# 5x5 depthwise sums in PSUM instead of SBUF, the padded images filled by ACT, and gathers of 128 rows instead of 126

## The chip, the cores and the metric

One core of a Trainium2 chip runs the whole program. The metric is the device time of one execution in microseconds; the median of several unprofiled and profiled executions is quoted. TensorE is PE below, VectorE DVE, ScalarE ACT, GpSimd POOL, SyncE SP.

## The reference, cut to what matters

Four images of 256 channels and 64x64 points go through four residual layers, each after a group norm:

```python
# layer 0: conv 1x1, depthwise 3x3 -> offsets and masks; 36 bilinear samples per point (4 groups x 9 points),
#          weighted sum, projection, squeeze-excite, fc1/fc2
samp = _grid_sample(img, sg)
dout = (samp * mr).sum(-1) ...
# layer 1: linear attention on q, k, v and on their 5x5 depthwise aggregation
qkv = relu(conv1x1(x) * scale + bias)                        # 768 channels
agg = conv2d(qkv, agg_dw_w, [(2, 2), (2, 2)], groups=C3) + agg_dw_b[None, :, None, None]
agg = conv2d(agg, agg_pw_w, groups=C3) + agg_pw_b
ms = concatenate([qkv, agg]);  vk = v @ k^T;  out = vk @ q / (sum(k) . q + eps);  proj, relu
# layer 2: binary 3x3 convolution        # layer 3: non-local attention with pooled keys
```

Layer 0's sampling is done by indirect DMAs (gathers) that POOL issues, each fetching one table row of 1 KB per partition. Layer 1's 5x5 aggregation is done by DVE: 25 multiply-adds of 128x1024 elements for each of 24 sums per image (here called accumulations: 2,400 in all, of which 2,304 are `scalar_tensor_tensor`; the first of each sum is a `tensor_scalar`). While image n is sampled, the remaining layers of image n-1 run beside it.

## The kernel before

The parts that the change and the argument touch:

```python
def depthwise(self, acc, src, w, k, rows, cols, r0, bias=None):
    for t in range(k * k):
        s = src[:, r0 + t // k:r0 + t // k + rows, t % k:t % k + cols]
        wt = w[:, t:t + 1]
        if t:
            nc.vector.scalar_tensor_tensor(acc, s, wt, acc, ALU.mult, ALU.add)
        elif bias is not None:
            nc.vector.tensor_scalar(acc, s, wt, bias, ALU.mult, ALU.add)
        ...

def sample(self, n, ssum):                       # 74 units an image, a unit is up to 4 rounds
    ...
            wm = self.gp.tile([P, UR, 4 * G, OB], F32, name="wm")        # bufs=2: weights of a unit
            ... nc.vector.tensor_tensor(wm[0:k, v0:v1], self.con("own")[0:k]..., sl[0:k, u + v0:u + v1, G:]..., ALU.mult)
            acc = self.ps2.tile([P, UR, P], F32, name="acc", tag="ps2")
            for v, (r, m) in enumerate(unit):
                k = m * PT                                               # 14 points x 9 = 126 rows
                g = self.gp.tile([P, G, 256], F32, name="g", bufs=8)
                for i in range(G):
                    nc.gpsimd.indirect_dma_start(out=g[0:k, i, :], ..., in_=table, in_offset=... sl.bitcast(I32)[0:k, r, i:i + 1])
                ... matmuls acc <- wm[0:k], g[0:k]
            ...
            yield 1

# layer 1
    def padded(tiles, b_loop): ...               # qkv, 8 blocks an image
            nc.scalar.activation(v, ps, AF.Relu, ...)
            nc.vector.tensor_copy(pd[:, 2 + 8 * b:10 + 8 * b, 2:W + 2], rw(v))
    def aggregate(pd, i, c, name):
        acc = bp.tile([P, 16, W], F32, name=name, tag=name)              # SBUF, "ak" or "av", bufs=2
        self.depthwise(acc, pd, self.w5[:, i], 5, 16, W, 16 * c, bias=self.b5[:, i:i + 1])
        return acc
    ...
        for c in range(4):
            ak = aggregate(kp, 2 + t, c, "ak")...; nc.scalar.activation(ak, ak, AF.Relu, ...)
            av = aggregate(vp, 4 + t, c, "av")...
            ...
            yield 56

def run(self):
    ...
        for i, _ in enumerate(self.sample(n, ssum), 1):
            while spent < i * SHARE:             # SHARE = 24: how much of the image before goes with a unit
                cost = next(before, None)
                ...
```

The order in which a built program's instructions stand on each engine is not that of the source: a scheduler at build time fixes it, from the source order and the dependencies.

## Time and profile before

| | before |
|---|---|
| unprofiled, 3 runs | 11,089.57 us median (11,062.62 to 11,095.54) |
| the profiled run that came with it | 11,979.3 us span |
| PE, DVE, ACT, POOL busy | 58%, 43%, 15%, 49% |
| sampling of images 0 to 3 | 1,751, 2,319, 2,374, 2,429 us |
| without gathers after images 1 and 2 / after image 3 | 428, 425 / 2,010 us |

The lines themselves are shown in the prediction. Read them by stage: whenever POOL is at work one image is sampled, and what the other engines do then is overlap; what lies in the stretches without POOL is paid in full.

### The profile page before, as it was taken

How to read it: one execution, taken by the hardware profiler on the slowest of the kernel's cores; microseconds unless marked ns; L12 is line 12 of the kernel's file. 1: busy time of each engine (PE TensorE's matmuls, PEld its weight loads, DVE VectorE, ACT ScalarE, POOL GpSimd, SP SyncE). 2: the span in 40 equal slices, each digit the busy share in tenths (PEclk: the TensorE clock that was granted, in tenths of full speed). 3: DMA queues.
4: the chain of work that ended last, by engine and by line, in shares of the span. 5: the costliest groups of instructions: out<-in, count | busy, mean ns of one | idle time of the engine just before them, and what ended most of it. 6: DMA issues, size and time to landing. Idle time of an engine off the chain costs nothing. (4 is left out here: it accounts for less than half of the span.)

```text
span 11979.3 us, 87750 instructions
## 1 busy us (share of the span) xinstructions
PE 6993.4 (58%) x34360; PEld 3582.5 (30%) x34360; DVE 5198.2 (43%) x6141; ACT 1794.6 (15%) x3153; POOL 5874.1 (49%) x4694
## 2 busy tenths in 40 slices
PE   3455434845466864664466866383447777832686
PEld 2222222322222342332222334242222334421235
DVE  5213200287462125256664023537657112399713
ACT  1110000111111121121111022021111012221002
POOL 1777776678764421478876350538877451000000
PEclk6665556866667887776566978596667788965698
DMA  3443433322322212322232122322232221100000
GB/s 108 123 125 102 125 95 92 96 64 73 87 67 70 65 43 81 102 66 76 77 85 83 42 75 67 107 71 60 64 84 72 65 71 42 53 0 0 0 10 14
DMA packets 687911, 838.70 MB, mean 70 GB/s; under 512 B 401289, under 2 KB 507145, under 8 KB 685705
## 3 DMA queue, kind: packets, MB, share of 16 engines
q0 software_dynamic: 299776, 604.62, 18.1%
q1 hardware_dynamic: 387720, 228.48, 6.6%
q8 instruction: 270, 4.42, 0.2%
q14 instruction: 145, 1.18, 0.0%
HBM read 731.68 MB, written 100.71 MB: 69 GB/s over the span
## 5 line engine op out<-in xcount | busy, mean ns | idle before, releaser
L411 POOL DMA_INDIRECT g<-tab,sl x4688 | 5873.4, 1253 | 4094.8 <-issue 1996.5
L418 PE MATMUL acc<-g,wm 126*32 126x128 f32 x18752 | 1600.9, 346 | 1387.6 <-issue 741.3
L418 PEld LDWEIGHTS acc<-g,wm 126*32 126x32 f32 x18752 | 819.3, 133 | 2196.3 <-issue 1272.5
L158 DVE SCALAR_TENSOR_TENSOR av<-pd,vec,av 128x1024 f32<-128x1024 f32 x1152 | 1473.0, 1279 | 2.1
L158 DVE SCALAR_TENSOR_TENSOR ak<-pd,vec,ak 128x1024 f32<-128x1024 f32 x1152 | 1470.6, 1277 | 0.5
L403 DVE TENSOR_TENSOR wm<-con,sl 126x1024 f32<-126x1024 f32 (+1 forms) x296 | 358.0, 1211 | 2150.7 <-remote 1622.4
L634 PE MATMUL ps<-xp,w 128*128 128x512 f32 x2304 | 1029.0, 606 | 12.7 <-issue 9.5
L424 PE MATMUL dp<-ident,at 128*128 128x128 f32 x1172 | 274.8, 375 | 1032.8 <-ACT at L421 646.2
L421 ACT COPY at<-acc 128x512 f32<-128x512 f32 (+1 forms) x296 | 171.8, 581 | 3525.8 <-remote 2319.9
L634 PEld LDWEIGHTS ps<-xp,w 128*128 128x128 f32 x2304 | 443.2, 194 | 575.9 <-issue 571.0
L424 PEld LDWEIGHTS dp<-ident,at 128*128 128x128 f32 x1172 | 180.0, 188 | 1180.1 <-ACT at L421 727.4
L549 PE MATMUL pt<-ident,ak 128*128 128x128 f32 x256 | 85.6, 390 | 723.6 <-ACT ak L565 723.6
L484 PE MATMUL ps<-x2f,f 128*128 128x512 f32 x1024 | 469.6, 615 | 15.1 <-ACT hm L485 11.1
L638 DVE TENSOR_TENSOR x<-x,ps 128x512 f32<-128x512 f32 x64 | 44.0, 688 | 957.3 <-PE ps L634 879.6
L490 PE MATMUL ps<-hm,f 128*128 128x512 f32 x1024 | 445.2, 593 | 0.0
L524 PE MATMUL ps<-xn,qw 128*128 128x512 f32 x768 | 393.5, 649 | 4.2 <-ACT xn L124 3.9
L431 ACT COPY dT<-dp 64x224 f32<-64x224 f32 (+1 forms) x592 | 199.4, 337 | 1268.2 <-PE dp L424 756.6
L320 PE MATMUL ps<-mw,t 128*128 128x108 f32 x512 | 129.1, 407 | 419.2 <-DVE t L142 344.2
L713 PEld LDWEIGHTS ps<-gt,pT 128*128 128x128 f32 x2048 | 310.6, 232 | 121.5 <-DVE pT L710 63.2
L696 PE MATMUL s<-ph,th 128*128 128x512 f32 x512 | 332.8, 738 | 2.3 <-issue 2.2
L708 PE MATMUL pt<-ident,pe 128*128 128x128 f32 x1024 | 161.4, 302 | 287.1 <-ACT pe L702 271.1
L713 PE MATMUL ps<-gt,pT 128*128 128x128 f32 x2048 | 306.8, 314 | 37.1 <-DVE pT L710 36.8
(190 smaller groups left out, 7610.3 us busy)
## 6 DMA issues: line engine op xcount, KB each, us to landing
g<-tab,sl POOLq DMA_INDIRECT x4688
x<-in_x SPq DMA_DIRECT2D x64, 512.0 KB
tab<-xo SPq DMA_DIRECT2D x512, 64.0 KB
y<-yc SPq DMA_DIRECT2D x32, 512.0 KB
x2f<-x SPq DMA_DIRECT2D x32, 512.0 KB
ybf<-y SPq DMA_DIRECT2D x32, 512.0 KB
out<-res SPq DMA_DIRECT2D x64, 256.0 KB
yb<-y SPq DMA_DIRECT2D x32, 504.0 KB
```

The source lines that it names most:

```text
L158: nc.vector.scalar_tensor_tensor(acc, s, wt, acc, ALU.mult, ALU.add)
L403: nc.vector.tensor_tensor(wm[0:k, v0:v1], self.con("own")[0:k].unsqueeze(1).unsqueeze(1).to_broadcast(sh), sl[0:k, u + v0:u + v1, G:].unsq ...
L411: nc.gpsimd.indirect_dma_start(out=g[0:k, i, :], out_offset=None, in_=table, in_offset=bass.IndirectOffsetOnAxis(ap=sl.bitcast(I32)[0:k, r ...
L418: nc.tensor.matmul(acc[32 * i:32 * i + 32, v, :], wm[0:k, v, 4 * i + 2 * x:4 * i + 2 * x + 2, :], g[0:k, i, x * P:(x + 1) * P], start=x == ...
L424: nc.tensor.transpose(dp[:, v].rearrange("p g s o -> p (g s o)"), at[:, v], self.ident)
L431: nc.scalar.copy(dT[hs, :, q0:q0 + m * (v1 - v0)].rearrange("p g (v o) -> p g v o", o=m), dp[hs, v0:v1, :, s, 0:m].rearrange("p v g o -> p ...
L484: nc.tensor.matmul(ps, f1[:, k, m * P:(m + 1) * P], x2[:, k], start=k == 0, stop=k == KT - 1)
L490: nc.tensor.matmul(ps, f2[:, k, m * P:(m + 1) * P], hm[:, k], start=k == 0, stop=k == 4 * KT - 1)
L524: nc.tensor.matmul(ps, qw[:, k, i * P:(i + 1) * P], xn[:, k], start=k == 0, stop=k == KT - 1)
L634: nc.tensor.matmul(ps, w[:, k, t, m * P:(m + 1) * P], xp[:, k, 8 * b + t // 3:8 * b + t // 3 + 8, t % 3:t % 3 + W], start=i == 0, stop=i = ...
L696: nc.tensor.matmul(s[:, i], tv[:, 4 * b + j], ph[:, i * 512:(i + 1) * 512], start=True, stop=True)
L713: nc.tensor.matmul(ps[:, 0:P], pT[:, m], gt[:, m], start=m == 0, stop=m == 7)
```

## The change

Its intent: beside accumulations with both inputs in SBUF a gather takes about 2.09 us where a free one takes 0.997 (the prediction has the lines, and the port on which the two are held to meet). With the sum in PSUM an accumulation has one SBUF input, which should end that. ACT, which has room, moves the sum out with the relu and fills the padded images. The PSUM banks for it come from the matmul pool (3 to 2). Gathers of 128 rows take in two rows of the next point; their product lands in an output column that is never copied out.

```diff
-        self.mm = e(tc.tile_pool(name="mm", bufs=3, space=PSUM))
+        self.mm = e(tc.tile_pool(name="mm", bufs=2, space=PSUM))
 ...
-                            out=g[0:k, i, :], out_offset=None, in_=table,
-                            in_offset=bass.IndirectOffsetOnAxis(ap=sl.bitcast(I32)[0:k, r, i:i + 1], axis=0))
+                            out=g[:, i, :], out_offset=None, in_=table,
+                            in_offset=bass.IndirectOffsetOnAxis(ap=sl.bitcast(I32)[:, r, i:i + 1], axis=0))
 ...   (wm and the matmuls likewise; s_d gets 252 rows of zeros at its end; sl is loaded for 128 rows)
-                        nc.vector.tensor_copy(pd[:, 2 + 8 * b:10 + 8 * b, 2:W + 2], rw(v))
+                        nc.scalar.copy(inner, rw(v))          # q: the relu itself writes into pd
 ...
-            def aggregate(pd, i, c, name):
+            def aggregate(pd, i, c, name, func, **more):
-                acc = bp.tile([P, 16, W], F32, name=name, tag=name)
+                acc = self.big.tile([P, 16, W], F32, name="agg", tag="big")       # bufs=1
                 self.depthwise(acc, pd, self.w5[:, i], 5, 16, W, 16 * c, bias=self.b5[:, i:i + 1])
-                return acc
+                v = bp.tile([P, 16, W], F32, name=name, tag=name)
+                nc.scalar.activation(v, acc, func, **more)
+                return v
 ...
-                    yield 56
+                    yield 28      (after the k sum, and again after the v sum)
 ...   (vk moves to a bank of ps1; the relu of the q sums goes from DVE to ACT)
```

More of the change, by code (lines that the diff above doesn't have):

```diff
@@ L194, in setup @@
         nc.vector.tensor_tensor(self.b5, self.b5, self.vec("agg_pw_b", n=6), ALU.add)
+        self.zero = cp.tile([P, TX * 2], F32, name="zero")
+        nc.vector.memset(self.zero, 0.0)
         dt = self.dp.tile
@@ L200, in setup @@
         self.x2_d = [dt([P, KT, HW], F32, name=f"x2{n}") for n in im]
-        self.s_d = [dt([HW * PT, G * 5], F32, name=f"sd{n}") for n in im]
+        self.s_d = [dt([HW * PT + 2 * RS, G * 5], F32, name=f"sd{n}") for n in im]
+        for n in im:
+            nc.sync.dma_start(self.s_d[n][HW * PT:].rearrange("(p r) f -> p (r f)", r=2), self.zero[0:RS, 0:G * 10])
         self.w2_d = dt([P, KT, 9, C], F32, name="w2")
-        self.zero = cp.tile([P, TX * 2], F32, name="zero")
-        nc.vector.memset(self.zero, 0.0)
     def binarise(self):
@@ L372, in coordinates @@
         nc.sync.dma_start(
-            self.s_d[n].rearrange("(t p q) f -> p t (q f)", p=P, q=PT)[:, c * CT:(c + 1) * CT, :],
+            self.s_d[n][0:HW * PT].rearrange("(t p q) f -> p t (q f)", p=P, q=PT)[:, c * CT:(c + 1) * CT, :],
             sd.rearrange("p t q f -> p t (q f)"))
@@ L384, in sample @@
             whole, part = np_ // RP, np_ % RP
-            rows = self.s_d[n][p0 * PT:(p0 + np_) * PT, :]
-            nc.sync.dma_start(sl[0:RS, 0:whole], rows[0:whole * RS].rearrange("(r p) f -> p r f", p=RS))
-            if part:
-                nc.sync.dma_start(sl[0:part * PT, whole], rows[whole * RS:])
+            nr = whole + (part > 0)
+            rows = self.s_d[n][p0 * PT:p0 * PT + nr * RS, :].rearrange("(r p) f -> p r f", p=RS)
+            more = self.s_d[n][p0 * PT + RS:p0 * PT + (nr + 1) * RS, :].rearrange("(r p) f -> p r f", p=RS)
+            nc.sync.dma_start(sl[0:RS, 0:nr], rows)
+            nc.sync.dma_start(sl[RS:P, 0:nr], more[0:P - RS])
             yb = sp.tile([P, KT, BP], F32, name="yb")
@@ L397, in sample @@
                 wm = self.gp.tile([P, UR, 4 * G, OB], F32, name="wm")
-                ku = unit[0][1] * PT
-                full = sum(1 for _, m in unit if m == unit[0][1])
-                for v0, v1, k in ((0, full, ku), (full, nu, unit[-1][1] * PT)):
-                    if v0 < v1:
-                        sh = [k, v1 - v0, 4 * G, OB]
-                        nc.vector.tensor_tensor(
-                            wm[0:k, v0:v1], self.con("own")[0:k].unsqueeze(1).unsqueeze(1).to_broadcast(sh),
-                            sl[0:k, u + v0:u + v1, G:].unsqueeze(3).to_broadcast(sh), ALU.mult)
+                sh = [P, nu, 4 * G, OB]
+                nc.vector.tensor_tensor(
+                    wm[:, 0:nu], self.con("own").unsqueeze(1).unsqueeze(1).to_broadcast(sh),
+                    sl[:, u:u + nu, G:].unsqueeze(3).to_broadcast(sh), ALU.mult)
                 acc = self.ps2.tile([P, UR, P], F32, name="acc", tag="ps2")
                 for v, (r, m) in enumerate(unit):
-                    k = m * PT
                     g = self.gp.tile([P, G, 256], F32, name="g", bufs=8)
@@ L411, in sample @@
                         nc.gpsimd.indirect_dma_start(
-                            out=g[0:k, i, :], out_offset=None, in_=table,
-                            in_offset=bass.IndirectOffsetOnAxis(ap=sl.bitcast(I32)[0:k, r, i:i + 1], axis=0))
+                            out=g[:, i, :], out_offset=None, in_=table,
+                            in_offset=bass.IndirectOffsetOnAxis(ap=sl.bitcast(I32)[:, r, i:i + 1], axis=0))
                     for x in range(2):
                         for i in range(G):
-                            nc.tensor.matmul(acc[32 * i:32 * i + 32, v, :], wm[0:k, v, 4 * i + 2 * x:4 * i + 2 * x + 2, :],
-                                             g[0:k, i, x * P:(x + 1) * P], start=x == 0, stop=x == 1)
+                            nc.tensor.matmul(acc[32 * i:32 * i + 32, v, :], wm[:, v, 4 * i + 2 * x:4 * i + 2 * x + 2, :],
+                                             g[:, i, x * P:(x + 1) * P], start=x == 0, stop=x == 1)
                 at = sp.tile([P, UR, P], F32, name="at")
@@ L424, in sample @@
                     nc.tensor.transpose(dp[:, v].rearrange("p g s o -> p (g s o)"), at[:, v], self.ident)
-                for v0, v1, m in ((0, full, unit[0][1]), (full, nu, unit[-1][1])):
+                full = sum(1 for _, m in unit if m == RP)
+                for v0, v1, m in ((0, full, RP), (full, nu, unit[-1][1])):
                     for s in range(2):
@@ L524, in padded @@
                             nc.tensor.matmul(ps, qw[:, k, i * P:(i + 1) * P], xn[:, k], start=k == 0, stop=k == KT - 1)
+                        inner = pd[:, 2 + 8 * b:10 + 8 * b, 2:W + 2]
+                        bn = {"bias": self.vec("qkv_b", i), "scale": self.vec("qkv_s", i)}
+                        if not b_loop:
+                            nc.scalar.activation(inner, rw(ps), AF.Relu, **bn)
+                            continue
                         v = bp.tile([P, 512], F32, name="v", tag=f"v{len(got)}")
-                        more = {"accum_out": b_loop[0][:, b:b + 1]} if b_loop and not got else {}
-                        nc.scalar.activation(v, ps, AF.Relu, bias=self.vec("qkv_b", i), scale=self.vec("qkv_s", i), **more)
-                        nc.vector.tensor_copy(pd[:, 2 + 8 * b:10 + 8 * b, 2:W + 2], rw(v))
+                        more = {} if got else {"accum_out": b_loop[0][:, b:b + 1]}
+                        nc.scalar.activation(v, ps, AF.Relu, **bn, **more)
+                        nc.scalar.copy(inner, rw(v))
                         got.append(v)
@@ L533, in padded @@
                 return dst
-            def aggregate(pd, i, c, name):
-                acc = bp.tile([P, 16, W], F32, name=name, tag=name)
+            def aggregate(pd, i, c, name, func, **more):
+                acc = self.big.tile([P, 16, W], F32, name="agg", tag="big")
                 self.depthwise(acc, pd, self.w5[:, i], 5, 16, W, 16 * c, bias=self.b5[:, i:i + 1])
-                return acc
+                v = bp.tile([P, 16, W], F32, name=name, tag=name)
+                nc.scalar.activation(v, acc, func, **more)
+                return v
             for t in range(2):
                 ks = sp.tile([P, 2, NB], F32, name=f"ks{t}")
-                vk = self.big.tile([P, 2, 512], F32, name="vk", tag="big")
+                vk = self.ps1.tile([P, 2, P], F32, name="vk", tag="vk")
                 def outer(kind, kv, vv, first, last):
@@ L553, in outer @@
                     for j in range(2):
-                        nc.tensor.matmul(vk[:, kind, 0:P], kt[:, 0, j], kt[:, 1, j],
+                        nc.tensor.matmul(vk[:, kind], kt[:, 0, j], kt[:, 1, j],
                                          start=first and j == 0, stop=last and j == 1)
@@ L563, in layer1 @@
                 for c in range(4):
-                    ak = aggregate(kp, 2 + t, c, "ak").rearrange("p r w -> p (r w)")
-                    nc.scalar.activation(ak, ak, AF.Relu, accum_out=ks[:, 1, c:c + 1])
-                    av = aggregate(vp, 4 + t, c, "av").rearrange("p r w -> p (r w)")
+                    ak = aggregate(kp, 2 + t, c, "ak", AF.Relu, accum_out=ks[:, 1, c:c + 1]).rearrange("p r w -> p (r w)")
+                    yield 28
+                    av = aggregate(vp, 4 + t, c, "av", AF.Copy).rearrange("p r w -> p (r w)")
                     for i in range(4):
@@ L569, in layer1 @@
                         outer(1, ak[:, cs], av[:, cs], c + i == 0, c + i == 6)
-                    yield 56
+                    yield 28
                 for kind in range(2):
                     j = 2 * kind + t
-                    nc.vector.tensor_tensor(ln[:, j], vk[:, kind, 0:P], self.con("bd"), ALU.mult)
+                    nc.vector.tensor_tensor(ln[:, j], vk[:, kind], self.con("bd"), ALU.mult)
                     kk = sp.tile([P, 1], F32, name=f"kk{j}")
@@ L581, in layer1 @@
                 for t in range(2):
-                    v = aggregate(qp[t], t, c, ("ak", "av")[t])
-                    nc.vector.tensor_scalar(v, v, 0.0, None, ALU.max)
-                    aq.append(v)
+                    aq.append(aggregate(qp[t], t, c, ("ak", "av")[t], AF.Relu))
                     yield 28
```

## The prediction

> **What bounds the kernel now.** I read the page's busy times first, then a table of stretches cut where the stages change, then the gathers one by one in the timeline, and last the order in which the built program's instructions stand on each engine. No engine is near full over the span:
>
> ```profile
> span 11979.3 us, 87750 instructions
> PE 6993.4 (58%) x34360; PEld 3582.5 (30%) x34360; DVE 5198.2 (43%) x6141; ACT 1794.6 (15%) x3153; POOL 5874.1 (49%) x4694
> ...
> DVE  5213200287462125256664023537657112399713
> POOL 1777776678764421478876350538877451000000
> ```
>
> POOL (the gathers of the sampling) works into the 34th slice; then one image's remaining layers run without it. The stretches (start:end, length, then busy time and count per engine: PE, PEld, DVE, ACT, POOL; clock; DMA) show the loop over the four images:
>
> ```profile
> 243.00:1994.00 1751.00, 765.73 (x5422) 396.49 (x5422) 350.11 (x461) 155.97 (x312) 1275.49 (x1172) 0.59 0.40 110
> ...
> 4741.00:7115.00 2374.00, 1461.09 (x7439) 708.36 (x7440) 1122.77 (x1241) 344.52 (x620) 1545.83 (x1172) 0.72 0.28 77
> 7115.00:7540.00 425.00, 251.67 (x1143) 174.65 (x1142) 167.72 (x289) 104.03 (x168) 0.01 (x1) 0.82 0.19 57
> 7540.00:9969.00 2429.00, 1452.99 (x7435) 705.49 (x7435) 1122.76 (x1241) 344.47 (x620) 1570.02 (x1172) 0.71 0.27 75
> 9969.00:10209.00 240.00, 175.17 (x914) 127.41 (x914) 81.06 (x159) 64.73 (x113) 0.49 (x1) 0.92 0.09 35
> 10209.00:10445.00 236.00, 223.46 (x520) 99.41 (x520) 75.11 (x115) 45.92 (x68) 0.00 (x0) 0.97 0.15 48
> 10445.00:11382.00 937.00, 399.86 (x1028) 178.93 (x1028) 810.36 (x785) 148.51 (x242) 0.00 (x0) 0.64 0.00 1
> 11382.00:11648.00 266.00, 251.31 (x580) 110.73 (x580) 23.58 (x54) 11.59 (x17) 0.00 (x0) 0.97 0.02 9
> ```
>
> Sampling image 0 takes 1751 us alone. Sampling images 1 to 3 (2319, 2374 and 2429 us) carries the previous image's feed-forward, layer 1, layer 2 and part of layer 3 along; then some 425 us finish layer 3 and prepare the next image. From 9969 on image 2's layer 3 ends (240 us), and image 3 runs alone: feed-forward 236, layer 1 937, layer 2 266, layer 3 331. So the bound changes: gathers while sampling, DVE in layer 1 (810 of 937 us), PE in layer 2.
>
> While sampling runs beside layer 1, gathers and the 5x5 sums get in each other's way:
>
> ```profile
> 5325.38 15.68 POOL L411 DMA_INDIRECT g<-tab,sl  x1 [0.59 <-PE acc L418]
> 5341.36 44.61 POOL L411 DMA_INDIRECT g<-tab,sl  x1 [0.30 <-issue]
> 5386.27 2.03 POOL L411 DMA_INDIRECT g<-tab,sl  x1 [0.30 <-issue]
> 5388.60 1.00 POOL L411 DMA_INDIRECT g<-tab,sl  x1 [0.30 <-issue]
> ...
> L411 POOL DMA_INDIRECT g<-tab,sl x4688: 952/997/56565, 243.0 to 9968.5; - x196
> L158 DVE SCALAR_TENSOR_TENSOR av<-pd,vec,av 128x1024 f32<-128x1024 f32 x1152 | 1473.0, 1279 | 2.1
> L158 DVE SCALAR_TENSOR_TENSOR ak<-pd,vec,ak 128x1024 f32<-128x1024 f32 x1152 | 1470.6, 1277 | 0.5
> ```
>
> A free gather takes 0.997 us and starts every 1.30. Beside an unbroken row of sums (start to start 1.194 us) it takes about 2.09; two of these took 15.68 and 44.61. Taking every gather's excess over 0.997 us, I get about 1,200 us over the four images. That is what the change wants back.
>
> **What the Trainium skill says.** "SBUF — State Buffer", section "Who interferes with whom": a DVE instruction with two SBUF inputs contends with a GpSimd one that reads SBUF, under an exclusive lock; one with at most one SBUF input, outside the two-port modes, does not. The gathers read their indices from SBUF, and the lines above agree. "VectorE: DVE Perf Modes", section on the TRN2 errata, gives fixed costs of 58 cycles SBUF to SBUF and 120 from PSUM, 65 ns apart at 0.96 GHz. For a PSUM source this trace hardly agrees (the 512-wide add takes 688 ns with one PSUM input, 691 without); no DVE instruction here writes PSUM. "DMA: Bandwidth & Descriptors", section on why a DMA increments its semaphore by 16, derives the engine count from the largest divisor up to 16: 126 rows would use 14 engines, 128 all 16. The trace shows only that rows matter little to POOL: the 72-row gathers took about 0.955 us, the 126-row ones 0.997.
>
> **The change part by part.**
> *Gathers of 128 rows:* 0.042 us for 54 rows makes 0.002 us a gather, 7 us in all. Transfers may land earlier; 1,172 gathers at 1.30 us would still be 1,524 us an image. I count nothing.
> *Filling the padded images on ACT:* 192 DVE copies of 0.43 us go (82 us), and 32 relu passes of 0.68 (22). ACT has room.
> *Sums in PSUM:* 2,304 accumulations lose their second SBUF input, so the lock goes. For each I take 1.25 us from start to start: 1.194, some 0.025 because one chain replaces two alternating ones (the 3x3 chain runs at 1.21 to 1.23), and half of the skill's 65 ns. There is one two-bank accumulator, so at each of 24 sums per image DVE waits for ACT to empty it: 1.06 us measured for ACT's 1024-wide relu, some 1.5 with both hand-overs, 36 us an image.
> *One matmul bank fewer:* feed-forward has two matmuls to one eviction and stays PE-bound; I count nothing apart.
> *Order:* this decides. DVE is in-order, and each unit of sampling (16 gathers) has one weight build (wm) on DVE that cannot run until the matmuls of two units earlier are done. Before, the scheduler puts 20 accumulations between two wm in the first part of layer 1 (199 in 8 units of image 2), so sampling and layer 1 advance together. In the changed program, only five:
>
> ```
> 645 L402 TensorTensor wm<-con,sl 128x1024
> 646 L158 TensorScalarPtr agg<-pd,vec,agg 128x1024 x5
> 647 L402 TensorTensor wm<-con,sl 128x1024
> ```
>
> For image 1's sampling I count 305 accumulating instructions of 600 before the last wm; 295, and every matmul of den, num, layer 2 and layer 3, come after it. It is the same for the next two. A unit then offers 5 x 1.25 + 1.2 = 7.5 us of DVE work to 16 gathers that need at least 20.8: DVE must wait for POOL at every wm, and half of layer 1 and two whole layers fall out of the overlap.
>
> *Sum,* in microseconds of the profiled run. Sampling alone ran 320 gathers in 464.9 us (from 1407.8 on), 1.453 each; I use 1.45 where only five accumulations run beside it.
> - Image 0 ends at 1994, as before.
> - Image 1: the first 192 gathers, beside feed-forward, take 383 as before; 980 x 1.45 = 1421; together 1804. What is left of image 0: 295 x 1.25 = 369 of accumulation, 13 evictions 19, other DVE work 70, PE's trailing part and waits about 60, together 520; layer 2 266; layer 3 331; then preparation 182 (4559 to 4741 before, and after layer 3 in both orders). 1804 + 1299 = 3103, before 2747.
> - Image 2: its first 192 gathers took 473; 473 + 1421 + 1299 = 3193, before 2799.
> - Image 3: 473 + 1421 = 1894, then 1117 for the rest of image 2.
> - Last image alone: 236 + 987 + 266 + 331 = 1820, where layer 1's 937 gets 39 for PSUM and 36 for evictions, and loses 25 of copies and relu.
> Total 1994 + 3103 + 3193 + 1894 + 1117 + 1820 = 13,121 against 11,979: 1.095 times. The unprofiled runs take 11,090; with the same ratio, about 12,150.
>
> **The rivals.**
> *The freed port wins.* Suppose layer 1 still went along with sampling as before. By the start of every 128th gather of image 2, the 40 units from 5215 to 6422 took 1,207 us; with DVE (199 x 1.25 + 8 x 1.2 = 258 us) as the bound of the first eight and gathers at 1.45 us (186) as that of the other thirty-two they would take 258 + 4 x 186 = 1,002. That is 205 an image, 615 in all: 11,364 profiled, 10,520 unprofiled, faster by 5%. For it: the blocked gathers. Against it: the order is fixed in the program, and the built order of the kernel before agrees with its trace for all 6,141 DVE instructions.
> *Sampling in the chip's free run is quicker.* Profiled runs are 8% slower, I cannot tell where. At the floor of 1.30 for the 980 gathers the profiled sum falls by 441 to 12,680, and the result to about 11,740. Still slower.
> *PSUM writes are dear.* At 1.5 us an accumulation the 295 + 295 + 295 + 600 outside sampling cost 371 us more: 12,490. A waiting q stage with two matmul banks (PE 228 of 380 us there) points the same way.
>
> **Range and chances.** The order makes the direction nearly sure; the size hangs on the gather rate and the PSUM chain. Middle 12,150, eight in ten from 11,700 to 12,700. Faster by over 2%: 0.04; within 2%: 0.05; slower by over 2%: 0.91.
>
> **What would show it.** Right: gathers at 1.0 us beside the sums, none of tens of microseconds; sampling of images 1 to 3 down to about 1,800 to 1,900 us; then some 1,100 us without gathers before preparation; more idle time of DVE before wm; accumulations at 1.2 to 1.3 us. Wrong: gathers still stretched by PSUM sums; POOL free stretches as short as before; or a unit much below 20 us, which would say that gathers of 128 rows are issued faster.

## The result, and the profile after

| | before | after |
|---|---|---|
| median | 11,079.08 us (4 runs) | 12,283.40 us (12,276.73 to 12,285.84, 4 runs) |
| profiled run, span | 11,979.3 us | 12,284.1 us |

The change is slower: 1.1086 times, 95% interval 1.1066 to 1.1106. A ratio is the mean time of one kernel's fast runs over that of the other's in the same rounds, so it is not quite the ratio of the medians.

The slices of the changed kernel (40 equal parts, busy tenths):

```profile
DVE  5223013334584235333468235333347713488713
...
POOL 1777777777500005577730001477771000000000
```

POOL now works at an even 7 tenths and then stands still for three or four slices at a time. The stretches (start:end, length, then busy time and count of PE, PEld, DVE, ACT, POOL, clock, DMA share, GB/s):

```profile
243.00:1769.00 1526.00, 979.01 (x5508) 441.22 (x5508) 355.30 (x465) 159.91 (x320) 1159.49 (x1172) 0.61 0.45 128
1769.00:3297.00 1528.00, 1111.42 (x6224) 520.85 (x6225) 587.42 (x573) 264.04 (x516) 1150.27 (x1173) 0.67 0.40 113
3297.00:4632.00 1335.00, 828.03 (x2299) 409.58 (x2298) 656.67 (x782) 210.70 (x321) 0.34 (x1) 0.77 0.07 21
4632.00:6286.00 1654.00, 1158.76 (x6266) 545.52 (x6266) 667.71 (x690) 268.67 (x514) 1146.74 (x1172) 0.66 0.39 110
...
9276.00:10400.00 1124.00, 732.29 (x1981) 352.06 (x1981) 562.39 (x635) 167.14 (x259) 0.00 (x0) 0.78 0.02 8
10400.00:12284.00 1884.00, 1119.33 (x3216) 557.63 (x3216) 1071.45 (x1143) 331.47 (x524) 0.00 (x0) 0.77 0.03 12
```

Sampling an image with another beside it takes 1,528 us (before: 2,319), hardly more than alone. But what follows without gathers takes 1,335 us where it took 428. DVE does about half as much during the sampling as before (587 us in image 1's; 1,047 in the second profile of the kernel before, shown below). Its groups (busy us, mean ns of one, then the idle time before them and what ended most of it):

```profile
L409 POOL DMA_INDIRECT g<-tab,sl x4688 | 4604.8, 982 | 4669.5 <-DMA sl<-sd 2909.2
...
L158 DVE SCALAR_TENSOR_TENSOR agg<-pd,vec,agg 128x1024 f32<-128x1024 f32 x2304 | 2966.2, 1287 | 67.7 <-DVE agg L158 0.5
...
L402 DVE TENSOR_TENSOR wm<-con,sl 128x1024 f32<-128x1024 f32 (+1 forms) x296 | 358.8, 1213 | 2786.4 <-PE acc L416 2775.3
```

A mean gather takes 0.982 us (before: 1.253, and 1.235 in its second profile), so the blocking is gone: of the 939 gathers that started while a sum was running, none took 1.8 us or more (counted in the trace; 597 of 937 in the second profile of the kernel before). An accumulation into PSUM lasts 1.287 us (1.278 before). And DVE has stood idle 2,786 us ahead of a weight build (wm), waiting for the matmuls that free its buffer. (In the second profile of the kernel before it was 1,805 us:)

```profile
L403 DVE TENSOR_TENSOR wm<-con,sl 126x1024 f32<-126x1024 f32 (+1 forms) x296 | 358.0, 1210 | 1804.9 <-PE acc L418 1804.8
```

DVE's timeline of the changed kernel shows one such step after the other:

```profile
5482.44 1.23 DVE L402 TENSOR_TENSOR wm<-con,sl 128x1024 f32<-128x1024 f32 x1 [12.56 <-PE acc L416]
5483.58 6.58 DVE L158 SCALAR_TENSOR_TENSOR agg<-pd,vec,agg 128x1024 f32<-128x1024 f32 x5
5502.45 1.23 DVE L402 TENSOR_TENSOR wm<-con,sl 128x1024 f32<-128x1024 f32 x1 [12.28 <-PE acc L416]
5503.59 7.91 DVE L158 SCALAR_TENSOR_TENSOR agg<-pd,vec,agg 128x1024 f32<-128x1024 f32 x6
```

A build, five or six accumulations, then 12 us of waiting, every 20.0 us: sixteen gathers at 1.25 us. It also gives the pitch of the sums: five in 6.58 us, so (6.58 - 1.29) / 4 = 1.32 us from start to start, where the kernel before had 1.196.

### The profile page after: what moved, and what is told of

The parts are those of the page before. It is cut to its first block, busy times and chain, and to the rows that moved or that the text cites. A ratio compares the mean times of both kernels' runs of the same rounds, so it can differ in the third digit from the quotient of the medians.

```text
span 12284.1 us, 87611 instructions
## 1 busy us (share of the span) xinstructions
PE 7999.7 (65%) x34360; PEld 3833.1 (31%) x34360; DVE 5349.8 (44%) x5917; ACT 1921.6 (16%) x3345; POOL 4605.5 (37%) x4694
## 5 line engine op out<-in xcount | busy, mean ns | idle before, releaser
L409 POOL DMA_INDIRECT g<-tab,sl x4688 | 4604.8, 982 | 4669.5 <-DMA sl<-sd 2909.2
L416 PE MATMUL acc<-g,wm 128*32 128x128 f32 x18752 | 2625.9, 375 | 1818.0 <-DMA g<-tab,sl 1762.8
L158 DVE SCALAR_TENSOR_TENSOR agg<-pd,vec,agg 128x1024 f32<-128x1024 f32 x2304 | 2966.2, 1287 | 67.7 <-DVE agg L158 0.5
L416 PEld LDWEIGHTS acc<-g,wm 128*32 128x32 f32 x18752 | 1061.7, 134 | 3376.7 <-DMA g<-tab,sl 2989.1
L402 DVE TENSOR_TENSOR wm<-con,sl 128x1024 f32<-128x1024 f32 (+1 forms) x296 | 358.8, 1213 | 2786.4 <-PE acc L416 2775.3
L556 PE MATMUL pt<-ident,av 128*128 128x128 f32 x256 | 86.1, 377 | 448.5 <-ACT av L544 448.5
L604 PE MATMUL rden<-rd,con 64*128 64x512 f32 x256 | 264.7, 1136 | 153.7 <-DVE rd L598 153.7
L595 PE MATMUL den<-av,ld 128*64 128x512 f32 x64 | 47.8, 840 | 480.4 <-ACT av L544 480.4
L437 PE MATMUL po<-dT,ow 128*128 128x504 f32 (+1 forms) x576 | 317.4, 702 | 2.5 <-ACT dT L430 1.4
L158 DVE SCALAR_TENSOR_TENSOR t<-y,vec,t 128x1024 f32<-128x1024 f32 x256 | 316.5, 1286 | 0.4
```

The costliest lines, as they stand in the source:

```text
L402: nc.vector.tensor_tensor(wm[:, 0:nu], self.con("own").unsqueeze(1).unsqueeze(1).to_broadcast(sh), sl[:, u:u + nu, G:].unsqueeze(3).to_bro ...
L409: nc.gpsimd.indirect_dma_start(out=g[:, i, :], out_offset=None, in_=table, in_offset=bass.IndirectOffsetOnAxis(ap=sl.bitcast(I32)[:, r, i: ...
L416: nc.tensor.matmul(acc[32 * i:32 * i + 32, v, :], wm[:, v, 4 * i + 2 * x:4 * i + 2 * x + 2, :], g[:, i, x * P:(x + 1) * P], start=x == 0, ...
L437: nc.tensor.matmul(po[:, 0:np_], self.ow[:, k, m * P:(m + 1) * P], dT[:, k, 0:np_], start=k == 0, stop=k == G - 1)
L604: nc.tensor.matmul(pb, self.con("sel")[0:64, j * P:(j + 1) * P], rd, start=True, stop=True)
```

## The experiments

My theory: the loss is the order of DVE's instructions, by which layer 1 no longer advances with the sampling. The main rival: the PSUM sums with their evictions and the lost matmul bank cost it. Beside these stood the question what the 128 rows do, for which I had counted nothing.

All kernels gave correct results. Ratios are to the kernel before in the same call, on the same chip. "Order" is the number of accumulations that the built program has between the 12th and the 20th weight build of image 2 (the first part of layer 1). "Sums" says where they are kept and how many can be open (begun and not yet finished) at once; "tied" means that sums and weight builds were made to wait for each other. "Blocked" counts gathers of 1.8 us or more. Sampling is that of images 1 and 2; the gap is the time without gathers after image 2.

| kernel | rows | sums | order | chip | median us | ratio | sampling | gap | blocked |
|---|---|---|---|---|---|---|---|---|---|
| before (second profile) | 126 | SBUF, 2 open | 199 | 11 | 11,086 | 1 | 2,024, 2,194 | 410 | 746 |
| after | 128 | PSUM, 1 | 36 | not given | 12,283 | 1.1086 | 1,528, 1,654 | 1,333 | 25 |
| e1_rows128 | 128 | SBUF, 2 | 199 | 11 | 10,506 | 0.9477 | 1,865, 2,023 | 410 | 105 |
| e2_psum126 | 126 | PSUM, 1 | 36 | 11 | 12,553 | 1.1324 | 1,585, 1,716 | 1,332 | 95 |
| e3_gate | 128 | PSUM, 1, tied | 175 | 11 | 10,379 | 0.9365 | 1,816, 1,941 | 407 | 70 |
| e4_gate126 | 126 | PSUM, 1, tied | 175 | 11 | 10,558 | 0.9524 | 1,841, 1,973 | 406 | 123 |
| e5_sbuf5 | 128 | SBUF, 2, tied to five | 49 | 11 | 11,999 | 1.0819 | 1,554, 1,683 | 1,239 | 55 |
| e6_share32 | 128 | as e3, SHARE 32 | 175 | 11 | 10,616 | 0.9572 | 2,085, 2,212 | 215 | 59 |
| e8_mix | 128 | av SBUF, rest PSUM | 156 | 2 | 11,957 | 0.9971 | 2,281, 2,377 | 430 | 523 |
| e9_chain126 | 126 | SBUF, 1 | 46 | 2 | 13,195 | 1.0989 | 1,829, 1,916 | 1,307 | 222 |
| e10_sbuf_fill | 128 | SBUF, 2 | 157 | 2 | 11,687 | 0.9727 | 2,227, 2,326 | 425 | 132 |
| e11_mix_gate | 128 | as e8, tied | 200 | 2 | 11,986 | 0.9987 | 2,345, 2,401 | 425 | 364 |
| e12_gate_sbuf | 128 | SBUF, 2, tied | 198 | 0 | 11,885 | 0.9867 | 2,279, 2,379 | 426 | 121 |

The kernel before took 11,086 us on chip 11, 12,021 on chip 2 and 12,060 on chip 0.

### First call: the rows alone, the PSUM sums alone, the order put back

**e1_rows128:** the kernel before with the hunks of the diff that concern `sample`, `s_d` and the zeros, and nothing of layer 1.

> The kernel before with gathers of 128 rows and nothing else: sums stay in SBUF, order of DVE stays about 200 accumulations per 8 units of image 2. If the rows are worth nothing, as the prediction had it: 11,080 us within 1%. If they are what brought a gather's start-to-start time from 1.30 to 1.25 us: image 0's sampling of 1,172 gathers is 59 us shorter, in all 60 to 240 us, so 10,840 to 11,020. Blocked gathers of tens of us beside the sums must still be there. If the 126-row form is also why the profiled run of the kernel before was 8% longer than its unprofiled ones, this kernel's profiled span is within 1% of its unprofiled time; if the sums in SBUF or the long overlap are why, it is again 8% longer.

Measured: 10,506 us, 5.2% faster. More than either expectation. The change contained a clear gain.

**e2_psum126:** the other hunks alone: sums in PSUM, filling by ACT, two matmul banks, gathers as before.

> The changed kernel with gathers of 126 rows: sums in PSUM, five accumulations per unit as in the changed kernel. If the order makes the loss, unprofiled 12,283 plus at most 4 x 59 us for the gathers at 1.30 instead of 1.25 us, so 12,280 to 12,520; slower than the kernel before by 11 to 13%. If the 128-row gathers made the loss, it falls to 11,100 or below. If the 126-row form is why the profile of the kernel before is 8% long, then the profiled span here is well above the unprofiled time, about 13,100, which is the profiled sum of the prediction.

Measured: 12,553 us, 1.1324, just above what I expected. The loss is all there without the 128 rows, which bring 269 us of the changed kernel's time (12,553 to 12,283). The profiled span (12,541) equals the other runs, so 126 rows are not what made the first profile long.

**e3_gate:** the changed kernel, with the weight builds made to depend on the progress of layer 1. `own`, a constant, is rewritten by DVE with its own values after every sum:

```diff
-                    wm[:, 0:nu], self.con("own").unsqueeze(1)...
+                    wm[:, 0:nu], self.own.unsqueeze(1)...
                 self.depthwise(acc, pd, self.w5[:, i], 5, 16, W, 16 * c, bias=self.b5[:, i:i + 1])
+                nc.vector.scalar_tensor_tensor(self.own, acc[:, 0, 0:OB], 0.0, self.con("own"), ALU.mult, ALU.add)
```

> The changed kernel, sums in PSUM and gathers of 128 rows, with one tiny added DVE operation per 25-tap sum that makes the next weight build wait for that sum, so that layer 1 advances with the sampling again (150 to 175 accumulations in the first 8 units of layer 1, as before the change; all 600 before the last weight build). If the lost overlap is the cause: the stretches without gathers fall from 1,335 to about 425 us for images 0 and 1 and from 1,124 to about 240 for image 2, sampling of images 1 to 3 takes about 1,700 to 1,800 us with no gather of tens of us, and the time is about 10,000 to 10,500 us, faster than both kernels. If the PSUM sums themselves, their evictions by ACT or the lost matmul bank are the cause, the time stays near 12,000 us or DVE's accumulations take well over 1.29 us each.

Measured: 10,379 us. The stretches of this kernel for image 1 and what follows (columns as above):

```profile
1771.00:3587.00 1816.00, 1240.21 (x7482) 635.79 (x7483) 1086.10 (x1101) 377.46 (x682) 1175.04 (x1172) 0.81 0.35 97
3587.00:3995.00 408.00, 237.00 (x1042) 163.02 (x1040) 162.56 (x277) 97.02 (x156) 0.00 (x0) 0.82 0.20 60
```

Sampling takes 288 us more than in the changed kernel (1,816 to 1,528), but DVE does 1,086 us of work in it instead of 587, and 408 us are left instead of 1,335. The edit adds work and takes none away; it changes the order. It gives back 1,905 us, more than the whole loss. The changed kernel may have run on another chip. e2 and e4 (below), which differ from each other by the tie alone, ran on the same one, and there it gives back 1,995 us (12,553 to 10,558). This is the theory's main proof: PSUM sums, evictions and the missing bank are all still there, and the kernel is faster than before.

### Second call: the same from the other side, and the odd first profile

**e7_before_again:** the kernel before, unchanged.

> The kernel before, profiled once more, to see whether its first profile stands for it. Its first profiled run took 11,981 us where its unprofiled runs take 11,080, and in the stretch where it samples image 0 alone its gathers went at 1.45 us where two other profiled kernels, one of them with the same 126-row sampling code, went at 1.30. If the first profile was an odd run, this one has a span near 11,080 us, gathers at 1.30 us alone, and image 0's sampling done in about 1,610 us instead of 1,751. If profiling slows this kernel, the span is again near 11,980.

Measured: span 11,043.0 us (a single run, so of unknown state, but like the six unprofiled ones beside it). Its stretches:

```profile
242.00:1846.00 1604.00, 1002.06 (x5508) 447.64 (x5508) 353.60 (x465) 160.02 (x320) 1246.74 (x1172) 0.59 0.44 120
1846.00:3870.00 2024.00, 1453.63 (x7498) 694.96 (x7499) 1047.07 (x1134) 345.04 (x634) 1488.12 (x1173) 0.76 0.31 86
3870.00:4277.00 407.00, 233.08 (x1026) 162.00 (x1025) 161.78 (x277) 97.06 (x155) 0.43 (x2) 0.82 0.20 60
```

So profiling doesn't slow this kernel. The first profile shows another kind of execution: sampling alone took 1,751 us instead of 1,604. The third call told why. On chips 2 and 0 every kernel behaves like the first profile, on chip 11 every one like this. Look at a stretch in which image 0 is sampled alone, from 1410 to 1760 us. First e10 on chip 2 (POOL's busy time and count are the fifth pair):

```profile
1410.00:1760.00 350.00, 118.95 (x1024) 64.97 (x1024) 19.65 (x17) 20.11 (x47) 238.25 (x242) 0.55 0.34 95
```

The same stretch of e1 on chip 11:

```profile
1410.00:1760.00 350.00, 221.42 (x1215) 91.23 (x1216) 22.07 (x20) 24.91 (x59) 265.26 (x279) 0.53 0.38 108
```

And POOL's timeline in e10 (start, length, in brackets the idle time before):

```profile
1494.04 0.94 POOL L409 DMA_INDIRECT g<-tab,sl  x1 [0.30 <-issue]
1499.08 1.97 POOL L409 DMA_INDIRECT g<-tab,sl  x1 [4.09 <-remote]
1501.35 0.94 POOL L409 DMA_INDIRECT g<-tab,sl  x1 [0.30 <-issue]
```

The same gathers, 242 against 279 in 350 us. Most are as short as on chip 11, but 21 to 25 times in 320 gathers the next one starts more than 2 us later, mostly up to 6 (on chip 11 at most twice; "remote": POOL waits for a semaphore whose raising the profile does not show). The mean pitch of 320 gathers alone is then 1.44 to 1.47 us, with 126 rows as with 128; on chip 11 it is 1.305 and 1.258. The first profile had 1.453. What differs on those chips is not settled: the gathers' 4 KB packets last about the same (median 159 ns on chip 11, 159 to 164 on chip 2). But PE's waits differ. From 1450 to 1800 us of the kernel before (us in all, times, longest), in the first profile:

```profile
PE acc L418 <- issue: 68.4, 89, 2.4
POOL g L411 <- remote: 29.8, 12, 3.8
```

and in the second:

```profile
PE acc L418 <- DMA g<-tab,sl: 135.2, 218, 2.6
```

On chip 11 PE waits for the gathers to land. On the others it does so for some 4 us at most (from 1410 to 1760 us of each trace), and stands for 49 to 107 us for nothing that the profile shows ("issue"). In e10 the gather of 1499.08 comes after such a stretch, and PE then makes up 61 matmuls in 3.13 us. So the gathers probably wait for buffers that late matmuls still hold; why PE is late is open. The kinds of chip came in different calls, and only the kernel before ran on both, so chip and time are not separated. The chip of the first runs is not given; that the first profile came from such a chip, and the changed kernel's runs (gathers at 1.25 us alone) from one like chip 11, is inferred from the likeness, PE's waits included.

**e4_gate126:** the tied kernel with gathers of 126 rows (the same two lines as in e3, on e2).

> Sums in PSUM with the order tied as in the gated kernel, but gathers of 126 rows as in the kernel before: against the kernel before it differs in the place of the sums alone (with what belongs to it) at about the same order. If freeing the gathers from the sums is worth much by itself: well below 11,080; from 4 x 59 us of slower gathers on top of the gated kernel's 10,379 I get 10,480 to 10,620. If the 128 rows are what made the gated kernel fast and PSUM sums are worth nothing: 10,900 to 11,100.

Measured: 10,558 us, 0.9524. At 126 rows and with the overlap kept, sums in PSUM, with what belongs to them, are worth 4.8%. At 128 rows the step from e1 to e3 is worth only 10,506 to 10,379, 1.2%. The two gains of the change overlap, since both remove the same blocking.

**e5_sbuf5:** e1, with its accumulations tied to the weight builds in fives, so that the sums in SBUF get the changed kernel's order:

```diff
+                nc.vector.tensor_scalar(self.tick, wm[:, 0, 0, 0:1], 0.0, None, ALU.mult)      # after each wm
 ...   in the 25 taps:
+            if gated and t and t % 5 == 0:
+                yield 24
+                nc.vector.tensor_scalar(w[:, t:t + 5], w[:, t:t + 5], self.tick, None, ALU.add)
```

> The kernel of the first experiment, sums in SBUF and gathers of 128 rows (10,506 us), with its accumulations tied to the weight builds so that about 5 to 6 stand between two of them, as in the changed kernel. If the order alone makes the loss: about 12,300 us, within 300, and stretches of about 1,250 to 1,350 us without gathers. If PSUM sums in the changed kernel make it: below 10,900 us. Built so, 480 more tiny DVE operations, an estimated 50 us at most.

Measured: 11,999 us, 1.0819, and 1,239 us without gathers. No PSUM sum is in it, and the order costs 1,493 us against e1. Of these at most 127 us can be the edit's own work: 680 small DVE operations (384 on the weights, 296 ticks) with that busy time, more than the 50 us that I had estimated. The 284 us to the changed kernel come from the two gaps (96 and 94) and the end (2,830 to 3,008, 178), where DVE works through its sums: a median pitch of 1.325 us there, 1.196 here. Some 80 us of longer sampling in e5 go against them.

**e6_share32:** e3 with `SHARE = 32`.

> The gated kernel (10,379 us) with a larger share of the previous image's work per unit (32 instead of 24), so that layer 3 too comes within the sampling (all layer 2 additions stand before unit 56 instead of 70). If the 425 us without gathers after each sampling can be hidden: the stretches shrink to some 190 us, and the time is 9,800 to 10,200 us. If the chain of the previous image's layers is what binds, not the gathers: the sampling gets longer by what the stretches lose, and the time stays within 2% of 10,379.

Measured: 10,616 us, 2.3% slower than e3. The gap fell from 407 to 215 us, but sampling image 2 grew by 271. That is the second alternative, a little worse than the 2% I gave it: the chain of the other layers binds there, not the gathers.

### How the rows matter: gathers and sums in step

DVE and POOL beside each other in layer 1, in the timeline of the kernel before (second profile; rows of PE left out):

```profile
2296.15 1.28 DVE L158 SCALAR_TENSOR_TENSOR av<-pd,vec,av 128x1024 f32<-128x1024 f32 x1
2296.20 2.10 POOL L411 DMA_INDIRECT g<-tab,sl  x1 [0.30 <-issue]
2297.34 1.28 DVE L158 SCALAR_TENSOR_TENSOR ak<-pd,vec,ak 128x1024 f32<-128x1024 f32 x1
...
2298.54 1.28 DVE L158 SCALAR_TENSOR_TENSOR av<-pd,vec,av 128x1024 f32<-128x1024 f32 x1
2298.60 2.08 POOL L411 DMA_INDIRECT g<-tab,sl  x1 [0.30 <-issue]
```

And in the timeline of e1 (other engines left out):

```profile
2224.80 1.33 DVE L158 SCALAR_TENSOR_TENSOR av<-pd,vec,av 128x1024 f32<-128x1024 f32 x1
2224.87 0.95 POOL L409 DMA_INDIRECT g<-tab,sl  x1 [0.30 <-issue]
...
2226.05 1.33 DVE L158 SCALAR_TENSOR_TENSOR ak<-pd,vec,ak 128x1024 f32<-128x1024 f32 x1
2226.12 0.95 POOL L409 DMA_INDIRECT g<-tab,sl  x1 [0.30 <-issue]
```

With 126 rows a free gather cycle is 1.30 us and a sum's 1.196. They fall into a rhythm of one gather to two sums: 2.40 us from gather to gather, each 2.1 us long. With 128 rows the gather cycle is 1.25 us. Here it fits: the sum stretches from 1.28 to 1.33 us, its pitch from 1.196 to 1.25, and one gather goes with each sum; the gather's 0.95 us lie wholly inside the sum's 1.33. Of the gathers that started within 0.15 us of a sum's start in an unbroken row, 522 of 559 were blocked in the kernel before, 1 of 827 in e1. So two rows more, worth 0.05 us a gather alone, brought 580 us. That it is the rhythm and not the rows as such, e9 below shows: it has 126 rows and sums with two SBUF inputs, but at a pitch of 1.321 us, and its sums block hardly a gather. How the port is passed from one to the other within such a cycle the trace does not show; the two rhythms it does.

### Third call: one accumulator or two, and a candidate for the fastest

**e8_mix:** the changed kernel, with the sums called `av` left in SBUF, so that two are open at once:

```diff
+                if name == "av":
+                    acc = bp.tile([P, 16, W], F32, name=name, tag=name)
+                else:
                     acc = self.big.tile([P, 16, W], F32, name="agg", tag="big")
 ...   (and v is acc then; no copy)
```

> The changed kernel with one difference: in K/V the sums of v (av) stay in SBUF, those of k, and one of the two of q, in PSUM. So two accumulators are open at once, and the built order has 156 accumulations in the first 8 units of layer 1 of image 2 again instead of about 36, with nothing added to force it. If the loss of the change comes from having one accumulator, whose sums can only go one after the other: stretches without gathers of some 400 us instead of 1,335, pitch of the sums about 1.20 to 1.25 us instead of 1.325, and about 10,050 to 10,350 us. If sums in PSUM cost it as such, half of them still there: above 11,200.

Measured on chip 2: ratio 0.9971. The order came back by itself (156), the gaps are 428 and 430 us, the pitch of the sums is 1.195, so the first theory holds against 1.1086. But it missed my time (0.907 to 0.934 of the kernel before): 523 gathers are blocked again. Of 714 that started during a sum in SBUF 408 were blocked, of 291 during a sum in PSUM none. The sums keep to 1.195 here and do not stretch, and the gathers do not fall into step; why they stretch in e1 and not here is not shown.

**e9_chain126:** the kernel before, its sums made to run one after the other; nothing of the change is in it:

```diff
+                nc.vector.tensor_tensor(gb, z, self.b5[:, i:i + 1], ALU.add)
-                self.depthwise(acc, pd, self.w5[:, i], 5, 16, W, 16 * c, bias=self.b5[:, i:i + 1])
+                self.depthwise(acc, pd, self.w5[:, i], 5, 16, W, 16 * c, bias=gb)
+                nc.vector.tensor_scalar(z, acc[:, 0, 0:1], 0.0, None, ALU.mult)        # frees the next sum
```

> The kernel before (sums in SBUF, 126 rows) with its sums made to run one after the other: each begins with a bias that the one before has released. No PSUM sum, no other part of the change. Built so, about five accumulations stand between two weight builds (46 in the first 8 units of layer 1 of image 2), and 282 are left after the last one. If one chain instead of two is the cause: about 12,300 to 12,700 us, like the 12,553 of the PSUM kernel with 126 rows. If PSUM sums are needed for the loss: at most 0.125 us more for each of 2,304 accumulations, so below 11,400. Besides, gathers beside such a chain, whose pitch of 1.32 us leaves room for the gather's 1.30, should hardly be blocked (2.09 us) although the sums have two SBUF inputs, if blocking is a matter of the two pitches.

Measured on chip 2: 13,195 us, 1.0989. My figure in us was for the other kind of chip; as a ratio it was 1.11 to 1.15, so the loss is a little smaller than expected, and its shape is the expected one. Image 1's sampling and what follows:

```profile
1987.00:3816.00 1829.00, 895.71 (x6230) 476.60 (x6228) 620.11 (x652) 243.78 (x482) 1258.69 (x1173) 0.66 0.34 93
3816.00:5115.00 1299.00, 829.95 (x2380) 413.53 (x2380) 636.75 (x809) 202.65 (x315) 0.00 (x0) 0.78 0.07 21
```

One chain of sums instead of two is enough for the build to put five between two weight builds and for 1,299 us without gathers. Its pitch is 1.321 us in SBUF; PSUM's is 1.325. So the slower pitch belongs to one chain, each sum waiting for the one before, and not to PSUM. My expectation about the blocking came true as well: of 910 gathers that started while a sum was running 29 were blocked (in the second profile of the kernel before 597 of 937). The other 193 of its 222 blocked gathers are not the sums' doing: 139 started during a weight build, 43 during layer 0's own 3x3 sums.

**e10_sbuf_fill:** the changed kernel with all sums in SBUF (`acc = bp.tile(..., tag=name)`, relu in place).

> The changed kernel with all sums back in SBUF, two at a time: 128 rows, filling of the padded images by ACT and one matmul bank fewer stay. Against the kernel with 128 rows alone (10,506 us) it shows what the filling by ACT and the lost bank are worth. DVE loses 192 copies of 0.43 us and 32 relu passes of 0.68, 104 us in all, most of it in layer 1 where DVE binds: about 10,400, at most 10,500. If the lost bank costs something, it is above 10,506.

Measured on chip 2: 0.9727, the best there, though my figures as ratios were 0.938 to 0.947, so that is a miss. The order is there (157) with everything of the change but the PSUM sums: neither the filling by ACT, nor the lost bank, nor the finer `yield` spoils it. It can't be set against e1 in microseconds, as e1 ran on chip 11; whether the filling by ACT pays stays open. Against e8 on the same chip, all sums in SBUF are 2.3% better than half of them: 132 blocked gathers to 523, and a pitch of the sums beside gathers of 1.25.

**e11_mix_gate:** e8 with the tie of e3.

> The mixed kernel (sums of v in SBUF, the others in PSUM) with the order tied as in the gated kernel: the candidate for the fastest. If sums at a pitch of 1.20 to 1.25 us instead of the gated kernel's 1.325 shorten layer 1 by 600 x 0.08 to 0.12 us an image: 10,379 less 200 to 290, about 10,100 to 10,200 us. If half of the sums in SBUF block the gathers again: 10,300 to 10,500.

Measured on chip 2: 0.9987, so no gain over e8, and a miss (as ratios I expected 0.91 to 0.95); 364 gathers blocked.

**e12_gate_sbuf:** e3 with all sums in SBUF.

> The gated kernel with its sums back in SBUF, two at a time, and nothing else changed (128 rows, filling by ACT and the tie of the weight builds stay): what PSUM sums alone are worth at the same order. Chips differ by now: on the one where the kernel before takes 11,080 us the gated kernel took 10,379 (0.9365 of the kernel before), on the other, where gathers alone go at 1.46 us instead of 1.25 and the kernel before takes 12,021, the kernel with all sums in SBUF and no tie took 0.9727. On a chip of the first kind: if gathers of 128 rows and sums in SBUF fall into step at 1.25 us, sums at 1.25 instead of 1.325 us save 0.075 x 600 an image, so 10,150 to 10,300 (0.916 to 0.930); if the lock costs more than that, 10,400 to 10,600 (0.939 to 0.957). On a chip of the second kind: 0.96 to 0.98.

Measured on chip 0: 0.9867, a chip of the second kind and just outside what I expected for one (0.96 to 0.98). The tie costs some 1.4% against e10 (0.9727), though on two chips. What PSUM sums alone are worth at 128 rows on chip 11 stays unmeasured; the step from e1 to e3 (1.2%) contains the filling by ACT, the bank and the tie too.

**The fastest:** on chip 11 e3 (10,379 us), 6.4% faster than the kernel before and 15.5% faster than the changed one (10,379 to 12,283). On chips of the second kind e10 (0.9727), without PSUM sums; e10 has not run on chip 11, nor e3 on chip 2, so which is better in general is open.

## Why the prediction was right, point by point

**The order decides: right, and shown from both sides.** Put back, it gives 1,905 us (e3); spoiled without PSUM sums, it costs 1,493 (e5). What the prediction did not see is where the order comes from. It took it from the built program (305 of image 1's 600 accumulations before the last weight build; the trace has the same 305) and left the reason open. e9 and e8 give it: one PSUM accumulator lets only one sum run at a time, and the build then places five to six accumulations per unit; with two open it places some twenty. Why it does so is not shown, only that it follows.

**The stretches without gathers: right.** Predicted 1,299, 1,299 and 1,117 + 1,820; measured 1,335, 1,333 and 3,008. The rest is 36 + 34 + 71 = 141 us. Most of it is the pitch of the sums: I took 1.25, it was 1.325, which makes 295 x 0.075 = 22 us in each gap and 895 x 0.075 = 67 in the end, 111 in all; some 30 us stay unexplained. (A slip on the way: with 1.194 and 1.25, layer 1's PSUM term is 600 x 0.056 = 34 us, not the 39 that I added.) My 1.25 halved a PSUM fixed cost that is not seen; the larger term, 0.125 us for one chain instead of two, I had put at 0.025, after the 3x3 sums. But these have two accumulators that partly alternate, so they don't show a single chain. The profile of the kernel before did: the 63 times that two sums of one name follow each other, the second starts 1.320 us (median) after the first.

**The gather rate: mis-sized.** I took 1.45 us from the first profile; it was 1.25 in the runs that counted. Sampling of images 1 to 3 came to 1,528, 1,654 and 1,657 instead of 1,804, 1,894 and 1,894, 753 us less in all (570 of them in the last 980 gathers of each image, 183 in the first 192), and image 0's to 225 less. e9, which ran on a chip like the first profile's, took 1,829 and 1,916 with the same order. The working was good for that chip.

**The factor from profiled to unprofiled: wrong.** I multiplied 13,121 by 11,090 / 11,979, since "profiled runs are 8% slower, I cannot tell where". They are not; the profile was of a slower execution, and the changed kernel's profiled run is as long as its others. This took away 971 us where the gathers took away 978, and 141 came on top: 13,121 - 978 + 141 = 12,284. So the total was right to 1.1% (12,150 to 12,283) because one mistake stood in for another: the ratio between two executions of the slow kind was carried over to the quick kind.

**Gathers of 128 rows "count nothing": wrong.** They are worth 269 us in the changed kernel (e2 to after) and 580 in the kernel before (e1). I asked only how much longer or shorter a gather is, and never compared its cycle with the pitch of the sums.

**PSUM sums free the gathers: right.** None of 15 us or more is left in the changed kernel; three of 13 us, each the first of an image, remain, as in the kernel before.

**The rivals.** "The freed port wins", 10,520 us, is what happens once the order is kept: e4 measured 10,558. "Sampling in the free run is quicker" was true of the gathers, but its 11,740 applied the false factor as well; its sum without it, 12,680, is near e2's 12,553. "PSUM writes are dear" falls: 1.287 us, and no slower in pitch than a chain in SBUF.

## What to carry to other kernels

Before moving a chain of dependent operations to a scarcer memory, count how many chains can be open at once: one accumulator where there were two lost half of layer 1 and two whole layers from the overlap here (1,905 us), and nothing in the instructions' own durations shows it; read the built order. When two engines get in each other's way, compare their cycles: gathers at 1.30 us beside sums at 1.196 were blocked by the hundred; at 1.25 they were not where the sums stretched to 1.25 (e1), but were where these kept to 1.195 (e8). And run the kernel before once more beside the new one, on the same chip, before building on its profile.

## What the Trainium skill lacked or had wrong

- "VectorE: DVE Perf Modes", section on the drain that can't be avoided, reports eight copies that took as long with a semaphore after each as with one after the last, and says that the semaphore costs nothing extra there. It lacks what it costs when an operation needs the result of the one just before. Here every accumulation waits for its predecessor on the same accumulator. With one chain the pitch is 1.321 us in SBUF (e9) and 1.325 in PSUM (after); with two chains in turn it is 1.196 (before) and, one in PSUM and one in SBUF, 1.195 (e8). Waiting for the operation just before costs 0.125 us.
- The same page, section on the TRN2 errata, has 120 cycles of fixed cost from PSUM to SBUF against 58, and no row for an operation that accumulates in PSUM with its other input in SBUF. 128x1024 in fp32 took 1.287 us (SBUF: 1.278); the 65 ns between the two figures are not seen.
- "SBUF — State Buffer", section "Who interferes with whom", says that the order of issue decides who blocks. It lacks that the two cycles can lock: one gather to two sums at 2.40 us where the gather's own cycle is 1.30, one to one at 1.25 where it is 1.25, with sums of two SBUF inputs in both.
- "DMA: Bandwidth & Descriptors", section on why a DMA increments its semaphore by 16, gives 14 engines for 126 rows and 16 for 128. The gathers' packets agree: 28 of 4 KB and 14 of 1 KB with 126 rows, that is 14 shares of 9 rows, and 32 of 4 KB with 128, that is 16 shares of 8. It says nothing of what it means for POOL: 0.997 us a gather with 126 rows, 0.946 with 128.
- No page that I read says that chips differ in how soon gathers let POOL go on: 1.25 to 1.31 us from gather to gather on chip 11, 1.44 to 1.47 on chips 0 and 2, and 11,086 against 12,021 and 12,060 us for the same kernel.
